# Cross-attention block: the opening, the steady round and the end of one instruction list put into a new order

## The chip, the core and the metric

The kernel runs on one core of a Trainium2 chip. Its engines work from separate instruction lists and meet only at semaphores: TensorE (PE in the profile; PEld is its loading of weights), VectorE (DVE), ScalarE (ACT) and GpSimd (POOL) compute, and SyncE (SP) issues nearly all DMAs. The metric is the device time of one execution in microseconds; less is better.

## The reference

64 sequences; each has 256 rows of text (512 wide) and 256 rows of audio (384 wide). All is float32.

```python
text_p  = einsum('bld,dh->blh', H_l, W_text) + b_text      # 256 x 512
audio_p = einsum('bsd,dh->bsh', H_a, W_audio) + b_audio    # 256 x 512
Q = layer_norm(text_p, g1, beta1)
K = layer_norm(audio_p, g2, beta2)
alpha = softmax(einsum('blh,bsh->bls', Q, K) / sqrt(512))  # 256 x 256
H = einsum('bls,bsh->blh', alpha, audio_p)
H = einsum('blh,hk->blk', H, W_out) + b_out
out = layer_norm(H + H_l, g_out, beta_out)
```

## The kernel before

**What is computed how.** The audio and output weights are folded into one matrix (wao), so that the context is taken from the raw audio rows: z = alpha times c, then y = z times wao. The layer norms' means are taken out of the weights ahead of time. The products are cut into blocks whose sums and differences save products: `Thirds` (3 x 3 blocks; 15 products of 171 columns in place of more) for the K projection and for y, `Fork` (2 x 2 blocks; 7 products of 256 columns) for the Q projection, and in the rounds from 3 on the same scheme for the scores (`score_part`). The sums of inputs that they need are made by GpSimd: `Sides` (csum for K, zsum for y, seven steps each, one by `add(1)`), `SumX` (xsum, four steps), `query_step` (qsum, four) and `key_step` (ksum, three). Sums of results are made in PSUM by VectorE and ScalarE between the products. One matmul instruction of the program stands as two in the trace.

**The rounds.** Work on one sequence is spread over several rounds of a loop. Round b handles the projections of b + 2 (`k2`, `q2`) and the first Q product of b + 3 (`q3`), the scores of b (`at`), the context of b - 1 (`last`, `context_one`) and of b - 2 (`old`, `context_two`), the output product of b - 2 (`old.o`, called `y`) and the last layer norm of b - 3 (`settled`). Transposes go through memory: rows are stored (`store`, `store_e`), read back as blocks of 32 x 32 (`fetch`, `fetch_e`, four DMAs each), and VectorE turns the blocks (`turn`, `turn_e`, `turn_x`, `turn_c`).

**The order is the program's.** The scheduler is set to manual: each engine, and SP's queue of DMAs, carries out its instructions in the order of the statements. An instruction waits for what it reads, and for the readers of what it overwrites; all behind it on its engine waits too.

**The order inside Thirds**, for K and for y alike: `one` (two products into N), `copy_n1` (ACT), `start_t` (DVE, writes T), `two` (into M), `three` (into T, so it waits for `start_t`), `copy_t` (ACT), `start_l0` and `start_l1` (DVE, read M, write L), `four` (into T, M, L), `take_m` and `start_u` (DVE, read M, write U), `five` (into N, then M, then U). K leaves PSUM by `copy_n`, `copy_u`, `leave_middle`, `leave_ends`, `leave`, `middle_d`, `middle_sum`; y by `plus_ends`, `plus_middle`, `plus_n0` and four row sums `last_10`, `last_11`, `last_00`, `last_01` (each ends with a READ_ACCUMULATOR). `seed` writes the bias into M ahead of `two`. The banks M, L, T/U and N exist once and are used in turn by K and y.

**The order inside Fork:** `Fork.seed` writes R (ACT), `one` into R, `after_one` copies it, `seven` into q2 (cleared by `Fork.clear`), `after_seven` copies that, `six` into R, `start_q3` and `step_r` (DVE), `five` into R, `after_five` (DVE, reads R), `two`, `three` (into R) and `four`. Then `square`, `scales_of` (logarithm and exponential) and `normalise` on ACT, `store` and `fetch`.

**Around the rounds.** Ahead of the loop stand the loading, the first projections of sequences 0 and 1 in plain form (`Projection`), the turning of the weights (`turn_weights`), the folding (`fold_multiply`, `fold_evict`, `fold_bias`), and the block sums of the weights (`weight_sums`, `third_weights`). The loop runs over b = 0 to 61; a list of single statements serves b = 3 to 60, while b = 0, 1, 2 and 61 go through a shared body with conditions, which calls whole groups (`after_one`, `rest`, `sum_x`, `leave_plus`). Behind the loop the last sequences are finished with plain products (`multiply`, `multiply_half`, `multiply_halves`, `evict`, `evict_halves`), and the last alphas are transposed on TensorE (`transpose_e`). The weights' and the matmuls' own lines: 548 (Thirds), 721 (Fork), 806 and 867 (scores), 945 (context), 431 (plain projections), 244 (folding); VectorE's two-operand sums in Thirds, Fork and the scores all stand at line 532, the row sums at 691, `shift` at 1144, `settle` at 1153.

Of the kernel before, what the change touches and what calls it, by code (L numbers as in the profile page):

```python
# [22 lines left out]
def kernel(  # L23
# [1156 lines left out]
    def add_bias(b):  # L1180
        xb = x_rows[b]
        for t in range(LT):
            nc.gpsimd.tensor_tensor(xb[:, t, :], xb[:, t, :], bao_sb, ALU.add)
# [5 lines left out]
    c_turn = RowTurn(c_0, AC, "cT")  # L1189
    x_turn = RowTurn(x_0, DC, "xT")  # L1190
    k[0] = Projection("k", 0, c_turn.T, wa_sb, ba_sb, AC, ST, bank[0:2])
    q[0] = Projection("q", 0, x_turn.T, wt_sb, bt_sb, DC, LT, bank[2:4])
    keep_busy(6)
    c_turn.tile(0)
    c_turn.tile(1)
    for t in range(ST):
        k[0].multiply(t, [0])
    k[0].multiply(0, range(1, AC))
    k[0].multiply(1, [1])
    x_turn.tile(0)  # L1200
    k[0].multiply(1, range(2, AC))
    x_turn.tile(1)
    war = []
    for a in range(AC):
        pool, tag = (work, "eT") if a else (once, "e")
        war.append(pool.tile([P, HC, P], F32, tag=tag, name=f"war_{a}"))
        arrange(war[a], wa_sb[:, a, :], HC, nc.gpsimd.tensor_copy)
    mean_wa = means(wa_sb, AC, "mwa")
    k[0].evict(0)
    centre(wa_sb, mean_wa, AC)  # L1210
    for chunks in ([0, 1], [2, 3]):
        for t in range(LT):
            q[0].multiply(t, chunks)
    ba_row = ba_sb.rearrange("p (o h) -> p o h", o=1)
    bt_row = bt_sb.rearrange("p (o h) -> p o h", o=1)
    k[0].evict(1)
    mean_ba = means(ba_row, 1, "mba")
    mean_wt = means(wt_sb, DC, "mwt")
    mean_bt = means(bt_row, 1, "mbt")
    cT[1] = turn_c(1)  # L1220
    k[0].scales()
    centre(ba_row, mean_ba, 1)
    centre(wt_sb, mean_wt, DC)
    centre(bt_row, mean_bt, 1)
    turn_weights(0, 2)
    k[0].normalise()
    k[0].store()
    load_c(2)
    k[0].fetch()
    load_x(2)  # L1230
    k[1] = Projection("k", 1, cT.pop(1), wa_sb, ba_sb, AC, ST, bank[4:6])
    for t in range(ST):
        k[1].multiply(t, range(AC))
    turn_weights(2, 2)
    wt_blocks = weight_sums(wt_sb, DC // 2, "wtsum")
    q[0].evict(0)
    q[0].evict(1)
    q[0].scales()
    xT[1] = turn_x(1)
    xs_1 = SumX(xT.pop(1), nc.vector)  # L1240
    xs_1.add(1)
    k[1].evict(0)
    k[1].evict(1)
    Fork.clear()
    xs_1.add(2)
    bt_step = const.tile([P, H2], F32, tag="bt_step", name="bt_step")
    nc.vector.tensor_tensor(bt_step, bt_sb[:, :H2], bt_sb[:, H2:], ALU.subtract)
    xs[1] = xs_1.add()
    cT[2] = turn_c(2)
    Fork.seed()  # L1250
    q[0].normalise()
    q[0].store()
    load_c(3)
    q[0].fetch()
    k[1].square()
    fold_multiply(0)
    g1_sb, be1_sb, g2_sb, be2_sb, bac_sb = take_columns()
    for v in (g2_sb, be2_sb):
        nc.vector.tensor_scalar(v, v, scale, None, ALU.mult)
    q[1] = Fork(1, xs.pop(1), wt_blocks)  # L1260
    q[1].one()
    q[1].seven()
    q[1].after_one()
    q[1].after_seven()
    wa_t = const.tile([P, 11, WP], F32, tag="wa_thirds", name="wa_thirds")
    third_weights(wa_sb, wa_t, [0])
    k[1].scales()
    wa_blocks = third_weights(wa_sb, wa_t, [3])
    cs[2] = Sides(cT.pop(2), "csum").add()
    ba_delta = third_bias(ba_sb, "ba_delta")  # L1270
    third_weights(wa_sb, wa_t, [1], nc.vector)
    fold_multiply(1, 0, 2)
    q[1].six()
    q[1].after_six()
    third_weights(wa_sb, wa_t, [4], nc.vector)
    fold_evict(0)
    Thirds.seed_with(ba_sb)
    k[1].normalise()
    k[1].store()
    load_x(3)  # L1280
    k[1].fetch()
    fold_multiply(1, 2, 4)
    fold_evict(1)
    q[1].five()
    q[1].after_five()
    xT[2] = turn_x(2)
    third_weights(wa_sb, wa_t, [2], nc.vector)
    part = bias_parts()
    bias_rest(part, 1, 3)
    folds.append(p_at.tile([P, H], F32, tag="at", name="ps_fold"))  # L1290
    fold_multiply(2, 0, 2)
    q[1].rest()
    q[1].square()
    q[1].scales()
    xs[2] = sum_x(xT.pop(2))
    q[1].normalise()
    q[1].store()
    q[1].fetch()
    wao_room = const.tile([P, HC * H], F32, tag="wo", name="wao_thirds")
    wao_t = wao_room[:, : 11 * WP].rearrange("p (n h) -> p n h", n=11)  # L1300

    def last_rows(b):
        x_rows[b] = blk.tile([P, LT, D], F32, tag="xq", name=f"x_{b}")
        nc.sync.dma_start(x_rows[b], x[b].rearrange("(t p) d -> p t d", p=P))
        c_rows[b] = blk.tile([P, ST, DA], F32, tag="cq", name=f"c_{b}")
        nc.sync.dma_start(c_rows[b], c[b].rearrange("(t p) d -> p t d", p=P))

    done = None
    for b in range(B - 2):
        at = att[b] = att.get(b) or Attention(b)  # L1310
        settled, old, last = att.pop(b - 3, None), att.get(b - 2), att.get(b - 1)
        three = b + 3 < B
        fast = b > 2 and three
        soon = b > 1
        if fast:
            k2 = k[b + 2] = Thirds("k", b + 2, cs.pop(b + 2), wa_blocks, ba_sb, ba_delta)
            q2 = q[b + 2]
# [45 lines left out]
            if b + 4 < B: load_c(b + 4)  # L1363
# [508 lines left out]
```

## Time and profile before

| | us |
|---|---|
| median of 3 runs (lowest to highest) | 1368.44 (1367.55 to 1368.47) |
| the profiled execution | 1367.78 |
| its span, first to last instruction | 1365.9 |
| TensorE busy | 1342.8 |
| VectorE, ScalarE, GpSimd busy | 1157.5, 1161.8, 1171.5 |
| share of the DMA engines' time in queue 1 | 84.5% |

A line of the timeline gives the start in us, the time from the first start to the last end, engine, source line, operation, what is written and read, the shape, and how many instructions were merged; in brackets the idle time of the engine before it and what ended it. A line of the waits gives who waited for whom: total us, times, longest. A line of the stages gives the stretch, its width, then for PE, PEld, DVE, ACT and POOL the busy time and the number of instructions, then the granted clock, the DMA share and GB/s. A line of the DMA issues ends with KB each and the median us from issue to landing. In a line of the groups stand, behind the count, busy us and mean ns of one, then the idle time ahead of them. Ends of matmuls are modelled, and in the timeline they overlap the next start.

### The profile page before, as it was taken

What the parts mean: (1) busy time and instruction counts of PE and PEld (TensorE: products, weight loads), DVE (VectorE), ACT (ScalarE), POOL (GpSimd) and SP (SyncE); (2) the same over time, 40 slices, a digit from 0 to 9 for tenths busy, and PEclk for the clock granted to TensorE, in tenths of its full rate; (3) what the DMA queues carried; (4) which work ended last, traced back from release to release, by engine and by line L of the source; (5) the groups of instructions that cost most, each with busy time, mean ns of one, the idle gap of its engine ahead of it and who ended that gap; (6) DMA issues with size and microseconds to landing.
All of it is one profiled execution on the core that took longest, in us unless ns stands there. A gap on an engine that the chain in (4) does not pass through costs nothing.

```text
span 1365.9 us, 28598 instructions
## 1 busy us (share of the span) xinstructions
PE 1342.8 (98%) x8125; PEld 1244.8 (91%) x8125; DVE 1157.5 (85%) x2733; ACT 1161.8 (85%) x3188; POOL 1171.5 (86%) x1838
## 2 busy tenths in 40 slices
PE   9999999999999999999999999999999999999997
PEld 5789999999999999999999999999999999999985
DVE  6758888888888888889888888888888888888857
ACT  5688988888888888888888888888888888888874
POOL 5669988989989889889899889899899889989844
PEclk9999999999999999999999999999999999999999
DMA  9786888988998898898888888898889899889772
GB/s 227 202 236 184 255 229 238 254 235 236 249 250 239 251 244 239 249 245 242 248 243 234 249 234 247 232 247 256 233 243 257 232 248 253 235 239 260 210 241 90
DMA packets 449107, 322.15 MB, mean 236 GB/s; under 512 B 153781, under 2 KB 381621, under 8 KB 448950
## 3 DMA queue, kind: packets, MB, share of 16 engines
q1 hardware_dynamic: 448854, 320.20, 84.5%
q8 instruction: 66, 1.08, 0.4%
q14 instruction: 91, 0.75, 0.2%
q10 hardware_dynamic: 96, 0.13, 0.0%
HBM read 203.57 MB, written 116.65 MB: 234 GB/s over the span
## 4 chain that ended last, share of the span: by engine, by line
PE 78%; DMA 7%; ACT 6%; DVE 3%; issue 2%; POOL 2%; SPq 1%; DVEq 0%; ACTq 0%; POOLq 0%
PE ps_f L721 23%; PE ps_m L548 13%; PE ps_sc L867 11%; PE ps_z L945 9%; PE ps_n L548 8%; PE ps_u L548 7%; PE ps_l L548 4%; DMA qd<-qr 2%; DMA kq<-kd 2%; DMA kd<-kr 1%; DMA qq<-qd 1%; ACT qr L787 1%; SPq L73 1%; ACT junk L777 1%; ACT junk L451 1%
## 5 line engine op out<-in xcount | busy, mean ns | idle before, releaser
L343 POOL TENSOR_TENSOR csum<-csum,cT 128x256 f32<-128x256 f32 x310 | 195.5, 640 | 9.9
L343 POOL TENSOR_TENSOR zsum<-zsum,zT 128x256 f32<-128x256 f32 x305 | 196.4, 653 | 5.3
L721 PE MATMUL ps_f<-wtsum,xsum 128*128 128x256 f32 x756 | 193.6, 379 | 0.5 <-DVE ps_f L532 0.5
L945 PE MATMUL ps_z<-eT,c 128*128 128x256 f32 x768 | 186.4, 379 | 0.2 <-ACT e L896 0.2
L945 PEld LDWEIGHTS ps_z<-eT,c 128*128 128x128 f32 x768 | 140.3, 190 | 14.1 <-ACT e L896 0.6
L721 PEld LDWEIGHTS ps_f<-wtsum,xsum 128*128 128x128 f32 x756 | 138.0, 190 | 15.1 <-DVE ps_f L532 1.2
L518 ACT ACTIVATE kT<-kT,columns 128x256 f32<-128x256 f32 x256 | 145.0, 596 | 2.8 <-DVE kT L511 1.5
L518 ACT ACTIVATE qT<-qT,columns 128x256 f32<-128x256 f32 x256 | 145.2, 593 | 2.2 <-DVE qT L76 2.2
L343 POOL TENSOR_TENSOR csum<-cT 128x256 f32<-128x256 f32 x124 | 98.6, 795 | 50.4 <-DVE cT L76 50.4
L721 PE MATMUL ps_f<-wt,xT 128*128 128x256 f32 x504 | 129.4, 379 | 0.6 <-ACT ps_f L713 0.6
L867 PE MATMUL ps_sc<-kT,qT 128*128 128x128 f32 x928 | 122.3, 275 | 0.0
L1153 DVE SCALAR_TENSOR_TENSOR yr<-yr,rstd,beo 128x512 f32<-128x512 f32 x120 | 119.6, 998 | 0.0
L849 POOL TENSOR_TENSOR ksum<-kT 128x512 f32<-128x512 f32 x58 | 73.9, 1275 | 53.0 <-ACT kT L518 53.0
L867 PEld LDWEIGHTS ps_sc<-kT,qT 128*128 128x128 f32 x928 | 116.6, 192 | 0.0
L867 PEld LDWEIGHTS ps_sc<-ksum,qsum 128*128 128x128 f32 x696 | 100.6, 191 | 6.0
L532 DVE TENSOR_TENSOR ps_l<-ps_m,t 128x171 f32<-128x171 f32 x248 | 85.3, 344 | 24.4 <-PE ps_m L548 12.9
L867 PE MATMUL ps_sc<-ksum,qsum 128*128 128x128 f32 x696 | 105.9, 275 | 0.0
L511 DVE STREAM_TRANSPOSE kT<-kq 128x512 f32<-128x512 f32 x122 | 85.4, 701 | 23.3 <-DMA kq<-kd 20.7
L777 ACT ACTIVATE junk<-ps_f 128x512 f32<-128x512 f32 x126 | 74.3, 590 | 36.2 <-PE ps_f L721 35.9
L1144 DVE SCALAR_TENSOR_TENSOR yr<-yr,nm,go 128x512 f32<-128x512 f32 x124 | 102.9, 831 | 1.0 <-ACT junk L1025 1.0
L721 PEld LDWEIGHTS ps_f<-wt,xT 128*128 128x128 f32 x504 | 92.9, 190 | 11.4 <-ACT ps_f L713 0.9
L76 DVE STREAM_TRANSPOSE qT<-qq 128x1024 f32<-128x1024 f32 x64 | 79.5, 1242 | 18.2 <-DMA qq<-qd 17.4
(265 smaller groups left out, 4127.9 us busy)
## 6 DMA issues: line engine op xcount, KB each, us to landing
kd<-kr SPq DMA_DIRECT2D x64, 512.0 KB, 3.1
kq<-kd SPq DMA_DIRECT2D x256, 128.0 KB, 3.8
qd<-qr SPq DMA_DIRECT2D x64, 512.0 KB, 5.2
qq<-qd SPq DMA_DIRECT2D x256, 128.0 KB, 3.7
xq<-in_x_dram SPq DMA_DIRECT2D x252, 128.0 KB, 5.0
x<-in_x_dram SPq DMA_DIRECT2D x63, 512.0 KB, 4.4
out_dram<-yr SPq DMA_DIRECT2D x62, 512.0 KB, 5.5
cq<-in_ctx_dram SPq DMA_DIRECT2D x252, 96.0 KB, 2.3
```

The lines of the kernel that those rows point to most:

```text
L76: nc.vector.transpose(dst.rearrange("p k (b j) -> p b k j", j=SQ), src.rearrange("p b (k i) -> p b k i", k=chunks),)
L343: nc.gpsimd.tensor_tensor(*step)
L511: nc.vector.transpose(self.T.rearrange("p k (q t j) -> p t q k j", t=self.nt, j=SQ)[:, t], self.sq[:, t * NQ : (t + 1) * NQ].rearrange("p ...
L518: nc.scalar.activation(self.T[:, k, :], self.T[:, k, :], AF.Identity, bias=bet[:, k : k + 1], scale=gam[:, k : k + 1],)
L532: nc.vector.tensor_tensor(o, i0, i1, op)
L548: nc.tensor.matmul(place, lhsT=self.sides.of[n], rhs=self.weights[n], start=(n == 14), stop=True, skip_group_check=True,)
L721: nc.tensor.matmul(place, lhsT=side, rhs=w, start=False, stop=True, skip_group_check=True)
L777: nc.scalar.activation(junk, fork[t], AF.Square, scale=1.0 / math.sqrt(H), accum_out=self.var[:, t : t + 1],)
L867: nc.tensor.matmul(self.place(t, m), lhsT=self.qsides[n][:, c], rhs=self.ksides[n][:, c], start=False, stop=True, skip_group_check=True,)
L945: nc.tensor.matmul(ps, lhsT=c_rows[self.b][:, s, bass.ts(j, P)], rhs=self.eT[:, s, :], start=start, stop=(s == ST - 1), skip_group_check=True,
L1144: nc.vector.scalar_tensor_tensor(row, row, self.nm[:, t : t + 1], go_sb, ALU.add, ALU.mult)
L1153: nc.vector.scalar_tensor_tensor(self.y[:, t, :], self.y[:, t, :], self.r[t], beo_sb, ALU.mult, ALU.add)
```

## The change

No operation, size or buffer is changed in the rounds; statements are put into another order. (1) All that stands ahead of round 3 is one list of single statements, in which the work of the plain start and of rounds 0, 1 and 2 is interleaved; groups are taken apart (`xs[2].add(1)` four times in place of `sum_x`, `score(0, 1)` ... in place of `score(0, 8)`, `bias_rest` and `fold_multiply` step by step). (2) The steady round, b = 3 to 60, has a new order. (3) Round 61 and the end are one list as well, with `add_bias` taken tile by tile. Of the first part (names with _0, _1, _2 belong to rounds 0 to 2):

```diff
+    fold_multiply(2, 0, 1)
+    q[1].three()
...
+    k2_0.one()
+    k2_0.copy_n1()
+    k2_0.start_t()
...
+    q[1].two()
+    load_c(3)
+    q[1].four()
...
+    fold_multiply(2, 1, 2)
...
+    fold_multiply(2, 2, 3)
...
+    fold_multiply(1, 3, 4)
+    Fork.seed()
+    k[1].store()
+    k2_0.two()
+    k2_0.three()
...
+    q2_0.one()
...
+    k2_1.one()
...
+    at_0.score(7, 8)
+    scales_of(q2_0, k2_0, var_0)
+    k2_1.copy_n1()
...
+    k2_1.start_t()
...
+    k2_1.three()
...
+    at_1.score(7, 8)
+    last_1.context_one()
+    k2_2.two()
+    Fork.seed()
...
+    q2_2.one()
```

The steady round, old (whole in the listing above, from `if fast:`) and new, in the new one all that the prediction speaks of:

```diff
-            k2.three()
-            k2.copy_t()
...
-            settled.shift(0)
-            q2.five()
...
-            k[b + 1].turn([0])
-            k2.leave_middle()
-            k2.leave_ends()
-            k2.leave()
-            q2.after_five()
...
-            y.start_t()
-            q2.three()
...
-            k2.store()
-            load_c_rows(b)
...
-            q2.store()
+        k2.one()
+        old.context_two(0); old.context_two(1)
+        k2.copy_n1()
+        at.affine_queries(3)
+        if b + 4 < B: load_c(b + 4)
+        cT[b + 3] = turn_c(b + 3)
+        old.copy_two()
+        q2.seven()
...
+        cs[b + 3].add(1)
+        k2.start_t()
+        k2.three()
...
+        load_x_rows(b - 1)
...
+        old.start_products(n=1)
...
+        q2.start_q3()
+        if done: done.store()
...
+        k2.take_m()
...
+        k2.start_u()
+        k2.five()
+        k2.copy_n()
+        q[b + 1].turn()
+        at.score_part(1, 7)
+        q2.step_r()
+        q2.five()
+        last.fetch_e()
...
+        k2.leave_ends()
...
+        k[b + 1].turn([0])
...
+        k2.leave_middle()
+        k2.leave()
+        y.one()
+        q2.after_five()
+        load_c_rows(b)
+        k[b + 1].turn([1])
+        y.copy_n1()
+        at.copy_p7()
+        k2.middle_sum()
+        y.start_t()
+        y.two()
+        at.query_step(2)
+        k2.square(var[:, 2:], [0])
+        at.copy_p1()
+        settled.shift(0)
...
+        q2.four()
+        y.three()
...
+        at.score_part(6)
+        if b + 4 < B: load_x(b + 4)
+        at.add_p7(0)
+        y.copy_t()
+        settled.shift(1)
+        q2.two()
+        q2.three()
...
+        settled.settle(1)
...
+        at.add_p7(1)
+        y.four()
+        scales_of(q2, k2, var)
...
+        settled.settle(0)
+        q2.normalise([0])
+        at.score_part(2)
+        last.turn_e()
...
+        y.take_m()
+        at.score_part(4)
+        at.score_part(3)
+        y.start_u()
+        at.maxima()
+        q2.normalise([1])
+        y.five()
...
+        y.plus_ends(x_old)
+        Fork.seed()
...
+        k2.normalise([1])
+        k2.normalise([0])
+        last.context_one()
...
+        y.plus_middle(x_old, 1)
+        at.exponentials([1])
+        y.last_11()
+        y.last_01(x_old)
+        q2.store()
+        y.plus_n0()
...
+        y.last_10()
...
+        k2.store()
...
+        q3.one()
...
+        q2.fetch()
...
+        k2.fetch()
+        y.last_00()
+        at.store_e()
```

Of the end:

```diff
+    last.o.one()
...
+    at.multiply(0, bank[5])
+    last.o.start_t()
+    last.o.three()
...
+    at.multiply_half(1, bank[4], 0)
...
+    at.multiply_half(1, bank[4], 1)
...
+    end.context_one()
...
+    end.copy_one()
+    last.totals()
+    last.deviation(0)
+    end.copy_two()
+    end.start_output()
+    end.multiply(0, bank[0])
```

More of the change, by code (lines that the diff above doesn't have):

```diff
@@ L1223 @@
-    centre(wt_sb, mean_wt, DC)
-    centre(bt_row, mean_bt, 1)
-    turn_weights(0, 2)
-    k[0].normalise()
-    k[0].store()
[L1228 to L1236, printed above, removed]
+    ba_row = ba_sb.rearrange('p (o h) -> p o h', o=1)
+    mean_ba = means(ba_row, 1, 'mba')
@@ L1278 @@
[L1278 to L1292, printed above, removed]
+    q[1].six()
+    q[0].store()
+    g1_sb, be1_sb, g2_sb, be2_sb, bac_sb = take_columns()
+    fold_multiply(0, 3, 4)
@@ L1297 @@
-    q[1].store()
-    q[1].fetch()
[L1299 to L1306, printed above, removed]
@@ new lines @@
+    at_1.score(0, 1)
+    k2_1.copy_u()
+    k2_2 = k[4] = Thirds('k', 4, cs.pop(4), wa_blocks, ba_sb, ba_delta)
+    k2_2.one()
+    at_1.affine_queries(2)
+    at_1.affine_queries(3)
+    last_1.store_e()
+    k2_1.leave_middle()
+    at_1.affine_keys(1)
+    k2_2.copy_n1()
+    q2_1.after_five()
+    q2_1.three()
+    beo_sb = row(beta_out, 'beo')
+    k2_1.middle_d()
+    at_1.score(1, 2)
+    q2_1.two()
+    k[2].fetch()
+    k2_1.leave_ends()
+    at_1.affine_keys(2)
+    at_1.score(2, 3)
```

1313 lines of the change are left out of this document (780 added, 533 removed).

## The prediction

> **What bounds the kernel now.** I read the page's head first, then the busy times by stage, then the timeline of TensorE, and last who waits for whom.
>
> ```profile
> span 1365.9 us, 28598 instructions
> ...
> PE 1342.8 (98%) x8125; PEld 1244.8 (91%) x8125; DVE 1157.5 (85%) x2733; ACT 1161.8 (85%) x3188; POOL 1171.5 (86%) x1838
> ```
> ```profile
> 7.00:102.00 95.00, 89.36 (x391) 66.32 (x390) 64.17 (x127) 68.39 (x173) 60.34 (x102) 1.00 0.87 225
> 102.00:1296.00 1194.00, 1191.07 (x7427) 1126.03 (x7426) 1045.17 (x2493) 1047.88 (x2901) 1079.69 (x1682) 1.00 0.87 241
> 1296.00:1357.00 61.00, 56.87 (x293) 48.36 (x291) 41.37 (x102) 41.27 (x107) 27.42 (x42) 1.00 0.53 166
> ```
> TensorE (the first number behind the width) is the bound in every stage, at full granted clock. The reader is to see that there is little to win: the change keeps every matmul, so only TensorE's pauses, its start and what follows its last matmul can shrink. How large they are is seen in its timeline:
>
> ```profile
> 102.11 0.45 PE L548 MATMUL ps_n<-wa,csum 128*128 128x171 f32 x2
> ...
> 277.92 1.13 PE L721 MATMUL ps_f<-wt,xsum 128*128 128x256 f32 x4 [0.54 <-DVE ps_f L532]
> ...
> 607.37 1.03 PE L721 MATMUL ps_f<-wtsum,xT 128*128 128x256 f32 x4
> 608.23 0.61 PE L867 MATMUL ps_sc<-ksum,qsum 128*128 128x128 f32 x4
> ...
> 617.40 0.31 PE L548 MATMUL ps_n<-wa,csum 128*128 128x171 f32 x1
> ...
> 637.86 0.31 PE L548 MATMUL ps_n<-wa,csum 128*128 128x171 f32 x1
> ...
> 1295.86 0.31 PE L548 MATMUL ps_n<-wa,csum 128*128 128x171 f32 x1
> ...
> 1355.75 1.46 PE L1107 MATMUL ps_u<-wao,zT 128*128 128x256 f32 x6
> ```
> A round begins with `k2.one()` (ps_n<-wa,csum). From 617.40 to 637.86 is 20.46 us without a pause. The 58 rounds written as one list (b = 3 to 60) run from 102.11 to 1295.86, that is 1193.75; at 20.46 they would be 1186.7, so **7.1 us** are lost in them, on some rounds only. A pause costs more than the idle time shown: four products are shown as 1.03 but the next starts 0.86 after them (0.17 of drain), and behind a pause they take 1.13 (0.10 of refill), so some 0.25 is added to each. Ahead of round 3 the idle time is 95.00 - 89.36 = 5.6, in nine pauses, so **7.9 us** are lost; in the last stage 61.00 - 56.87 = 4.1 in five pauses, **5.4 us**. Behind the last matmul (1355.75 + 1.46 = 1357.2) stand 8.7 us.
>
> ```profile
> PE ps_u L548 <- DVE ps_u L532: 7.9, 7, 1.5
> ```
> ```profile
> 1311.35 0.53 PE L548 MATMUL ps_u<-wao_thirds,zsum 128*128 128x171 f32 x2 [1.40 <-DVE ps_u L532]
> ...
> 1327.85 0.53 PE L548 MATMUL ps_u<-wao_thirds,zsum 128*128 128x171 f32 x2 [1.53 <-DVE ps_u L532]
> ...
> 1339.55 0.53 PE L548 MATMUL ps_u<-wao_thirds,csum 128*128 128x171 f32 x2 [0.64 <-DVE ps_u L532]
> ```
> Seven of the pauses are one wait: `three()` needs `start_t`, which needs ACT's `copy_n1`, which needs `one()`. Three lie in the tail (1.40 + 1.53 + 0.64 = 3.6), so the other four, 4.3, lie in the first rounds.
>
> **The first three rounds.** Up to the products of `q[0]` TensorE's list is the old one. The new lists put each `one`, `copy_n1`, `start_t` well ahead of its `three`: between `k2_0.one` and `k2_0.three` stand two products, three folds and `two` (about 4.9 us of TensorE, a 256-wide product of four matmuls being 0.86), between `k2_1.one` and its `three` eight score steps, and so on. The copy (0.3), `start_t` (0.34) and two hops need about 1 us once ACT is free. All four waits go: 4.3 + 4 x 0.25 = 5.3. The remaining 2.6 (five pauses) I neither credit nor charge in detail: the new order also has places without reserve. `Fork.seed` must wait for squares, logarithm, exponential and normalise behind `four`, about 3 us of ACT; the order leaves 3.4 us of TensorE there in round 0 and over 4 in the others. And `last_1.context_one` now comes in round 1 ahead of the fork's first product, behind a store and a fetch of e. Bounds: from all 7.9 gone to 2 us worse; value taken -5.4, since the waits named are surely broken up and the new ones look short.
>
> **The steady round.** Its pauses (the row at 277.92 is one) are `q2.three` waiting for `after_five`, which stands on DVE behind the first half of the kT transpose:
>
> ```profile
> DVE kT L511 <- DMA kq<-kd: 20.7, 24, 1.8
> ...
> DVE qT L76 <- DMA qq<-qd: 17.4, 34, 1.0
> ```
> ```profile
> SPq L73 <- DMA qd<-qr: 48.7, 62, 3.5
> ```
> ```profile
> kd<-kr SPq DMA_DIRECT2D x64, 512.0 KB, 3.1
> kq<-kd SPq DMA_DIRECT2D x256, 128.0 KB, 3.8
> qd<-qr SPq DMA_DIRECT2D x64, 512.0 KB, 5.2
> qq<-qd SPq DMA_DIRECT2D x256, 128.0 KB, 3.7
> ```
> ```profile
> 618.61 1.90 SPq L73 DMA_DIRECT2D kq<-kd  x4
> ...
> 621.37 1.92 SPq L73 DMA_DIRECT2D qq<-qd  x4
> 624.49 2.98 SPq L73 DMA_DIRECT2D eq<-ed  x4
> ...
> 635.84 0.38 SPq L489 DMA_DIRECT2D kd<-kr  x1
> 636.32 0.42 SPq L101 DMA_DIRECT2D c<-in_ctx_dram  x1
> 636.79 0.87 SPq L489 DMA_DIRECT2D qd<-qr  x1
> ```
> ```profile
> 623.83 0.71 DVE L511 STREAM_TRANSPOSE kT<-kq 128x512 f32<-128x512 f32 x1
> ...
> 626.77 1.25 DVE L76 STREAM_TRANSPOSE qT<-qq 128x1024 f32<-128x1024 f32 x1
> ...
> 629.41 0.30 DVE L532 TENSOR_TENSOR ps_sc<-ps_sc,sc 128x128 f32<-128x128 f32 x1 [0.54 <-PE ps_sc L867]
> ```
> Counting from the round's start (617.40): the k fetch is issued from 1.2 to 3.1, lands some 3.8 later, and is wanted at 6.4, so nothing is in reserve. DVE is late by up to 1.8, TensorE stands from about 0.5 on. The new order turns q first (at 5.7, behind `start_u`), the first half of k at 7.7, and moves `q2.three` from 9.3 to 12.3. `load_c_rows` leaves its place between the two stores. `y.three` (10.7) becomes the first product to feel a late k; its `start_t` ends at about 10.2, and DVE idles 0.4 ahead of `after_five`. So k may land at 8.3 instead of 6.9, 1.4 later, for the same issue times: that covers nearly all lateness seen. I take 1.0 of the 7.1 as left, a gain of 6.1; bounds 0 to 7.1 for this cause.
>
> The moves that I cost at nothing are these. On SP the list becomes `load_c`, `load_x_rows`, the output store, `last.fetch_e`, `load_c_rows`, `load_x`, the q and k stores, the q and k fetches, `store_e`; it is the same 26 transfers. SP waits for the q store's landing about where it waited before, with only the k fetch and the e store behind it, and the rows that the five loads bring are used a round later: a round of 20.46 us hides them. If that cover went, `turn_c`, now the first long DVE work of a round, would hold `start_t` and `three` one for one. The e fetch (now at 7.1, 624.49) stays near 7 to 10, since the e store still goes out at about 3, and `turn_e` comes at about 15: some 4 us cover it. On ACT the q rows' normalise moves ahead of k's, and `Fork.seed` ahead of both k halves, which only eases the next `q3.one`; `copy_p1` moves behind a square and must end ahead of the sixth score part (11.0), about 10.7 by my layout, the smallest reserve on ACT. On POOL one csum step moves ahead of the zsum chain:
>
> ```profile
> L343 POOL TENSOR_TENSOR zsum<-zsum,zT 128x256 f32<-128x256 f32 x305 | 196.4, 653 | 5.3
> ```
> A step is 0.65 at the mean, so the fifth zsum step ends at about 7.5 and `y.one` starts at 8.7: covered by 1 us, and a shortfall would count in full.
>
> With these durations laid end to end, two places are narrow. First, `last_10` moves behind `last_11` and `last_01`; it frees the bank that the next `k2.one` writes:
>
> ```profile
> 635.25 0.51 DVE L532 TENSOR_TENSOR n<-ps_m,x 128x342 f32<-128x342 f32 x1 [0.54 <-PE ps_m L548]
> ...
> 636.79 0.51 DVE L691 SCALAR_TENSOR_TENSOR yr<-ps_n,n 128x342 f32<-128x342 f32 x1
> 637.23 0.08 DVE L691 DVE_READ_ACCUMULATOR yr<-ps_n,n 128x1 f32 x1
> ```
> From 17.85: two sums (0.43 and 0.24), two row sums of 0.44 and 0.42, `plus_n0` 0.37, `last_10` 0.34: free at 20.1. TensorE wants it about 0.22 ahead of 20.46, so 0.1 is left; with 0.12 of hand-over at each row sum it would be 0.1 late. Taken at 0, bound 58 x 0.1 = 6 us. The second is the third rival below.
>
> **The tail.** All three `three` waits get other products between (for `last.o` a whole `at.multiply(0)`, 2.6 us): -(3.6 + 3 x 0.25) = -4.3. Against it, `at.multiply_half`, which until now filled the time of the last `copy_two`, is moved ahead of `end.context_one`, and `end.copy_two` still stands on ACT behind `last.deviation(0)`; TensorE then has nothing until `end.multiply(0)`. Copy and hops alone are 0.6; if the deviation is late, 1.3 or more. I charge 1.0, and 0.8 for the longer DVE list ahead of the last evictions. Net -2.5; bounds -4.5 to +1. The 8.7 us behind the last matmul keep the same steps.
>
> **Sum.** The profiled execution took 1367.78, 1.9 more than its span; the median shown is 1368.44, 0.66 above it. 1367.78 - 5.4 - 6.1 - 2.5 = 1353.8, and as a median **1354.4 us**.
>
> **The rivals.** *The q fetch comes too late (slower).* q is turned 3.7 us earlier in the round (626.77 is 9.4), ahead of `step_r`, and `q2.five` (7.8) needs that. The new ACT order finishes q at about 16.5, ahead of k, so the store goes out at 16.55 instead of 19.4. With the store's landing time L, the last of four fetches is issued 1.5 behind it and lands 3.7 later: 1.3 + L in the next round. At L = 3.1, as for kd into an idle queue, that is 4.4: in time. At L = 5.2, as for qd now, it is 6.5: 0.8 late, of which 0.3 is absorbed, and 58 x 0.5 = 29 us are lost: 1383. It decides from L = 4.7 on. For it speaks that the row says 5.2; against, that those 5.2 stand behind kd and the c rows, which the new order puts behind q.
>
> *The rounds win nothing* (another hop takes the place of `after_five`, or the bank above is late): 1354.4 + 6.1 = 1360.5. For it speak the 0.1 and 0.3 us reserves; against, that most rounds already run at 20.46 with reserves like these.
>
> *Lengthened DVE work (slower).* `settle(1)`, `settle(0)` and `turn_e` now stand ahead of `take_m` and `start_u`, which the third pair of `y.five` (17.0) needs by 16.75.
>
> ```profile
> 618.06 1.01 DVE L1153 SCALAR_TENSOR_TENSOR yr<-yr,rstd,beo 128x512 f32<-128x512 f32 x1
> ...
> 630.62 1.21 DVE L1144 SCALAR_TENSOR_TENSOR yr<-yr,nm,go 128x512 f32<-128x512 f32 x1
> ...
> 631.96 0.73 DVE L1153 SCALAR_TENSOR_TENSOR yr<-yr,rstd,beo 128x512 f32<-128x512 f32 x1
> ```
> The same instruction takes 0.73 or 1.01, and the shift 0.74 to 1.21, depending on what runs beside it. From `add_p7(0)` at 11.7 (629.41 is 12.0; the sixth part comes 0.3 earlier) the chain ends at 16.2 with the short times and at 17.2 with the long ones: 0.4 late, 58 x 0.4 = 23 us, 1377. POOL should idle from about 12.7 until `key_step(0)`, so I expect it short. The Trainium skill ("SBUF — State Buffer") states that VectorE and GpSimd share one port pair under an exclusive lock, and that a VectorE instruction with two SBUF inputs contends with a GpSimd instruction that reads SBUF. The two durations of one instruction above agree; which engine was ahead the row does not say.
>
> *The start wins nothing* (the e fetch or the seeds replace the old waits): 1354.4 + 5.4 = 1359.8.
>
> **How the numbers follow.** The forecast gets 0.56, rounds without gain 0.12, start without gain 0.10, both together (about 1366 to 1368) 0.06, late q 0.09, lengthened DVE 0.07. A difference under 0.2% (2.7 us) can't be told from none. Faster: 0.56 + 0.12 + 0.10 = 0.78; same 0.06; slower 0.16. The likeliest case has 1349 to 1360; to hold 8 in 10 the range reaches over the partial cases, to a slight loss: 1349 to 1372.
>
> **What would show it.** Right: rounds of 20.46 from first to last, no `three` wait on ps_u above 0.3, kq and qq waits of DVE gone or harmless, a new wait for the last zT copy near the end. Wrong: a wait that comes back in every round: ps_f behind `step_r` (late q), ps_m in `y.five` (long DVE work), ps_n at the round's start (bank), each visible as a longer round; or pauses in the first 100 us of the old sum.

## The result, and the profile after

The changed kernel takes **1348.77 us** (median of 4 runs, 1348.47 to 1349.4), the kernel before beside it 1368.45: a ratio of 0.9857 with the interval 0.984 to 0.9874, 19.7 us less. Forecast were 1354.4 with a range of 1349 to 1372; the time lies 0.2 below the range. The direction came as forecast, the gain was 5.6 larger; of the reasons given, part held and part did not.

The profiled execution took 1349.4, and its page begins:

```profile
span 1347.6 us, 28668 instructions
...
PE 1337.4 (99%) x8125; PEld 1246.1 (92%) x8125; DVE 1114.9 (83%) x2733; ACT 1163.0 (86%) x3188; POOL 1140.3 (85%) x1838
```

The stretches (width, then busy time of PE, PEld, DVE, ACT, POOL), cut where the three lists meet, and the rows of TensorE's timeline at these cuts and at its end:

```profile
7.00:96.00 89.00, 88.11 (x391) 66.41 (x390) 61.57 (x127) 67.95 (x173) 61.41 (x104) 1.00 0.91 231
96.00:1284.17 1188.17, 1187.81 (x7426) 1126.70 (x7426) 1007.34 (x2496) 1050.03 (x2901) 1048.07 (x1681) 1.00 0.90 244
1284.17:1340.27 56.10, 56.10 (x293) 48.73 (x291) 40.59 (x101) 41.40 (x109) 27.58 (x42) 1.00 0.56 172
```
```profile
96.01 0.74 PE L548 MATMUL ps_n<-wa,csum 128*128 128x171 f32 x4
...
1284.16 0.59 PE L945 MATMUL ps_z<-eT,c 128*128 128x256 f32 x2
...
1338.81 1.46 PE L1107 MATMUL ps_u<-wao,zT 128*128 128x256 f32 x6
```

The instructions of TensorE are the same 8125, its granted clock is 1.00 as before, and in the last stretch it has no idle time at all (56.10 of 56.10). Round 3 begins at 96.01 (102.11 before), the list of round 61 at 1284.16 (1295.86), the last matmul ends at 1338.81 + 1.46 = 1340.27 (1357.2). That gives each stage its share:

| stage | before | after | difference | forecast |
|---|---|---|---|---|
| up to round 3 | 102.1 | 96.0 | -6.1 | -5.4 |
| 58 steady rounds | 1193.75 | 1188.15 | -5.6 | -6.1 |
| round 61 to the last matmul | 61.35 | 56.1 | -5.2 | } -2.5 |
| behind the last matmul | 8.7 | 7.3 | -1.4 | } |
| span | 1365.9 | 1347.6 | -18.3 | -14.0 |

Round 3 can also begin earlier than in this trace: seven traces of kernels with this list ahead of round 3 have its start at 94.07 to 96.08, at the mean 95.1.

Who waits for whom, first TensorE's list, then VectorE's waits for the fetches of e and k, and the DMA issues:

```profile
PE ps_f L187 <- POOL ones L111: 1.6, 1, 1.6
PE ps_m L244 <- issue: 0.6, 1, 0.6
...
PE ps_m L548 <- DVE ps_u L532: 0.2, 1, 0.2
```
```profile
DVE eT L76 <- DMA eq<-ed: 7.6, 7, 4.2
...
DVE kT L511 <- DMA kq<-kd: 0.6, 1, 0.6
```
```profile
kd<-kr SPq DMA_DIRECT2D x64, 512.0 KB, 2.9
qd<-qr SPq DMA_DIRECT2D x64, 512.0 KB, 2.8
kq<-kd SPq DMA_DIRECT2D x256, 128.0 KB, 3.1
qq<-qd SPq DMA_DIRECT2D x256, 128.0 KB, 2.7
...
eq<-ed SPq DMA_DIRECT2D x244, 64.0 KB, 5.0
```

The first row is the wait for a constant at the start, as before. The wait of ps_u ahead of `three`, 7.9 in seven pauses before, is gone. So are VectorE's waits for kq and qq (20.7 and 17.4): the 0.6 that is left for kq lies ahead of round 3. What is new is small: VectorE waits for the fetch of e seven times, once for 4.2 ahead of round 3 and six times in the steady rounds, for 3.3 together. The longest of the six, 0.96 at 869.68, reaches TensorE as the pause of 0.23 on ps_m in `y.five`, at 871.04. Of the 58 steady rounds, three of those with such a wait are longer than 20.46, by 0.16, 0.31 and 0.50. The q store lands in 2.8 where it took 5.2.

### The profile page after: what moved, and what is told of

It reads as the page before. It is cut to its first block, busy times and chain, and to the rows that moved or that the text cites. A ratio compares the mean times of both kernels' runs of the same rounds, so it can differ in the third digit from the quotient of the medians.

```text
span 1347.6 us, 28668 instructions
## 1 busy us (share of the span) xinstructions
PE 1337.4 (99%) x8125; PEld 1246.1 (92%) x8125; DVE 1114.9 (83%) x2733; ACT 1163.0 (86%) x3188; POOL 1140.3 (85%) x1838
## 4 chain that ended last, share of the span: by engine, by line
PE 98%; DVE 0%; SPq 0%; DMA 0%; issue 0%; ACT 0%; POOL 0%; DVEq 0%; POOLq 0%
PE ps_f L721 28%; PE ps_m L548 16%; PE ps_sc L867 13%; PE ps_z L945 12%; PE ps_n L548 11%; PE ps_u L548 8%; PE ps_l L548 5%; PE ps_sc L806 2%; PE ps_f L431 0%; DMA eq<-ed 0%; SPq L73 0%; PE ps_m L244 0%; PE ps_u L431 0%; PE ps_fold L244 0%; PE ps_l L244 0%; PE ps_n L431 0%
## 5 line engine op out<-in xcount | busy, mean ns | idle before, releaser
L343 POOL TENSOR_TENSOR csum<-csum,cT 128x256 f32<-128x256 f32 x310 | 220.4, 712 | 9.7
L343 POOL TENSOR_TENSOR zsum<-zsum,zT 128x256 f32<-128x256 f32 x305 | 167.5, 566 | 0.5
L1144 DVE SCALAR_TENSOR_TENSOR yr<-yr,nm,go 128x512 f32<-128x512 f32 x124 | 116.9, 943 | 0.7 <-ACT junk L1008 0.7
L867 PEld LDWEIGHTS ps_sc<-ksum,qsum 128*128 128x128 f32 x696 | 97.9, 191 | 3.1
L1008 ACT ACTIVATE junk<-yr,nm 128x512 f32<-128x512 f32 x124 | 89.8, 724 | 5.5
L343 POOL TENSOR_TENSOR csum<-cT 128x256 f32<-128x256 f32 x124 | 73.8, 595 | 23.0 <-DVE cT L76 22.8
L852 POOL TENSOR_TENSOR qsum<-qT 128x256 f32<-128x256 f32 x116 | 84.8, 731 | 6.1
L1153 DVE SCALAR_TENSOR_TENSOR yr<-yr,rstd,beo 128x512 f32<-128x512 f32 x120 | 89.4, 745 | 0.0
L314 POOL TENSOR_TENSOR xsum<-xT 128x256 f32<-128x256 f32 x124 | 89.0, 739 | 0.2 <-DVE xT L76 0.2
```

Of the source, the lines that this page charges most:

```text
L314: self.engine.tensor_tensor(*step)
L343: nc.gpsimd.tensor_tensor(*step)
L852: nc.gpsimd.tensor_tensor(*self.steps[n])
L867: nc.tensor.matmul(self.place(t, m), lhsT=self.qsides[n][:, c], rhs=self.ksides[n][:, c], start=False, stop=True, skip_group_check=True,)
L1008: nc.scalar.activation(junk, self.y[:, t, :], AF.Square, bias=self.nm[:, t : t + 1], accum_out=self.ssq[:, t : t + 1],)
L1144: nc.vector.scalar_tensor_tensor(row, row, self.nm[:, t : t + 1], go_sb, ALU.add, ALU.mult)
```

## The experiments

Three runs take one part of the change each, with the other two in the old order. The fourth undoes one suspected cause in the kernel before. Times are medians; the length of a stage is read from the one profiled execution of each kernel.

**The opening alone.** The new list ahead of round 3, then the old steady rounds and end.

> Everything ahead of round 3 in the new order, the steady rounds and the last stage in the old one. My theory (the three parts are independent, and each removes its own pauses of TensorE): ahead of round 3 the two traces differ by 6.2 us (102.1 against 96.0 us for the start of round 3), so this kernel is 5 to 7 us faster than before, about 1362.3, a ratio of 0.9955, and its 58 steady rounds still lose about 7 us. Rival (the parts lean on each other: the old steady round begins with whatever the new opening hands it, so a wait that left the opening returns in the first old rounds): under 3 us faster, with new pauses in rounds 3 to 5.

Measured 1360.17, ratio 0.9943 (0.9926 to 0.996): 8.3 less than the 1368.52 of before. Its stretch from 7 to 102 us:

```profile
7.00:102.00 95.00, 95.00 (x435) 73.40 (x434) 66.74 (x140) 73.86 (x190) 67.31 (x114) 1.00 0.92 235
```

TensorE has no idle time left there, and round 3 begins at 94.80, 7.3 earlier than before. No new pauses follow in the old rounds (1193.0 for the 58, 1193.75 before): the rival falls. The gain is above the 5 to 7 expected, in part because the expectation went by the opening of the changed kernel's trace, one of the slowest. Every pause of this stage is gone, not only the four that the prediction credited.

**The steady rounds alone.**

> Only the 58 steady rounds in the new order; the opening, round 61 and the last stage in the old one. My theory: the steady rounds lose 7.1 us before and 1.9 after, so this kernel is 4.5 to 6 us faster, about 1363.2, a ratio of 0.9962, with the waits of the kT and qT transposes for kq and qq gone from the DVE list and the lateness of `last_10` and of the long DVE work costing nothing. Rival (the steady round's gain in the changed kernel came from the opening's order of the queues and not from its own list): under 2 us faster, with the waits for kq still there.

Measured 1362.43, ratio 0.9958 (0.9943 to 0.9973): 6.1 less. VectorE's list has no wait for kq and none for qq any more; the one fetch for which it still waits is that of e:

```profile
DVE eT L76 <- DMA eq<-ed: 0.4, 2, 0.3
```

The theory holds, the gain being at its upper end: the new rounds win without the new opening.

**The end alone.**

> Only round 61 and the last stage in the new order; the opening and the 58 steady rounds in the old one. My theory: the last stage loses 5.4 us of TensorE before and 0.1 after, and what stands behind the last matmul is 8.7 before and 7.3 after, so this kernel is 6.6 us faster (6 to 7.5), about 1361.9, a ratio of 0.9952. Rival (the figure of the prediction, that a copy behind the last deviation holds TensorE up by 1.0 and the longer VectorE list by 0.8, masked in the one profile by chance): about 2.5 us faster.

Measured 1365.98 (1364.66 to 1368.46 in 10 runs), ratio 0.9986 (0.9977 to 0.9996): 2.5 less, the very number of the rival; the 6 to 7.5 of the theory were missed. The trace shows why it is no proof of the rival. A row of TensorE's timeline and one of VectorE's waits in round 61 of this kernel:

```profile
1307.94 0.85 PE L548 MATMUL ps_m<-wao,zsum 128*128 128x171 f32 x4 [2.95 <-ACT ps_m L562]
```
```profile
DVE qT L76 <- DMA qq<-qd: 4.4, 1, 4.4
```

The new list turns q early in round 61, but the old round ahead of it still fetches q late. VectorE stands for 4.4 with the sums of K behind it, ScalarE's write of the bias into M waits for these, and TensorE waits for that: 2.95. It is a price of the seam between two orders, which the whole change does not pay.

**The old kernel with one load moved.** In its steady round, only this:

```diff
             k2.store()
-            load_c_rows(b)
...
             q2.fetch()
+            load_c_rows(b)
             y.last_00()
```

> The kernel before with one transfer issue moved in the steady round: the load of the context rows, which stood between the store of k and the store of q, comes behind the fetch of q. Theory (the load of 512 KB between the two stores makes the q store, and with it both fetches, land late, and that lateness is what the steady pauses are): 3 to 5 us faster, a ratio of about 0.997, and the idle time of VectorE at kT<-kq falls from 20.7 us to under 8. Rival (the lateness is the place at which the order of VectorE wants k, 6.4 to 6.9 us into the round, and not the load): less than 1 us of change, ratio 0.9995 to 1.0005, and the idle time at kT<-kq stays between 15 and 25 us.

Measured 1361.56, ratio 0.9953 (0.9938 to 0.9968): 7.0 less than before, as much as all of the new steady round brings (6.1 alone; the two intervals overlap). The stretch of its steady rounds, VectorE's only wait of any size for the two fetches, and its DMA issues:

```profile
102.11:1289.00 1186.89, 1186.62 (x7422) 1126.06 (x7421) 1041.52 (x2488) 1044.27 (x2899) 1064.93 (x1682) 1.00 0.88 242
```
```profile
DVE qT L76 <- DMA qq<-qd: 1.8, 6, 0.5
```
```profile
kq<-kd SPq DMA_DIRECT2D x256, 128.0 KB, 2.7
qd<-qr SPq DMA_DIRECT2D x64, 512.0 KB, 3.8
```

TensorE is idle for 0.3 in 1187, and the 58 rounds take 1187.60 in place of 1193.75. In the new order they take 1187.14 to 1188.85 in seven traces, so beyond the moved load no gain of the new round can be told. The wait for kq is out of the list, k's fetch lands in 2.7 (3.8 before) and q's store in 3.8 (5.2). So the lateness of k came from this load (of 384 KB, not 512) between the stores; with it moved, the old place of the turn is late enough.

The next three start from the changed kernel. **The load put back** between its stores:

```diff
         q2.after_five()
-        load_c_rows(b)
...
         q2.store()
+        load_c_rows(b)
         y.plus_n0()
```

> The changed kernel with the load of the context rows put back between the two stores of the steady round (behind the q store, ahead of the k store). Theory (in the old order that load was the whole cause of the steady pauses; the new order was saved by moving it as much as by turning k later): the k store lands about 5.2 us behind its issue instead of 2.9, as the q store did behind the same load in the kernel before, so k lands near 8.0 us into the round where VectorE wants it at 7.6; part of the rounds pause again, 1.5 to 8 us slower than the changed kernel (about 1350 to 1357), with VectorE idle at kT<-kq for more than 5 us in total. Rival (the later turn of k, at 7.6 and not 6.4, is what removed the pauses, and covers the load too): within 0.7 us of the changed kernel.

Measured 1357.61 (1354.88 to 1358.73), 8.8 slower than the changed kernel. VectorE's waits for the fetches, TensorE's wait in the rounds, and the k store:

```profile
DVE eT L76 <- DMA eq<-ed: 24.5, 31, 4.0
...
DVE kT L511 <- DMA kq<-kd: 5.6, 13, 1.3
```
```profile
PE ps_m L548 <- DVE ps_u L532: 4.5, 7, 1.2
```
```profile
kd<-kr SPq DMA_DIRECT2D x64, 512.0 KB, 4.5
```

The store behind the load is again the slow one (k's now, 4.5). The loss is a little above the theory's 8; in the traces the steady rounds take 1195.57, 7.4 more than in the changed kernel and 1.8 more than in the kernel before. The way is as the theory had it only in part: k is late 13 times (once of them ahead of round 3), but the pauses of TensorE stand at `y.five`, since SP now waits for the k store in every round (64.8 in 58 waits, 3.4 in six without the load), so that it fetches e later too, and `turn_e` (late 31 times, once ahead of round 3) stands ahead of `take_m` and `start_u`. The new order tolerates this load no better than the old one did.

**The last copy first.** `end.copy_two` ahead of `last.totals` and `last.deviation(0)`.

> The changed kernel with the last `end.copy_two` ahead of `last.totals` and `last.deviation(0)` on ScalarE. Theory (the product `end.multiply(0)` starts with the two chunks that `copy_one` delivers and reaches the third only some 1.7 us later, so the copy was never late): no change, within 0.5 us, and the pause ahead of the product stays under 0.2. Rival (the prediction's: TensorE waits there for a copy behind a deviation, 1.0): 0.7 to 1.0 faster.

Measured 1347.81 (1347.61 to 1348.47), 1.0 less. By the time alone that is the rival. The rows of ScalarE and TensorE, first of the changed kernel, then of this one:

```profile
1334.20 0.59 ACT L961 COPY zT<-ps_z 128x512 f32<-128x512 f32 x1 [3.17 <-POOL nm L990]
...
1334.84 2.84 PE L1042 MATMUL ps_m<-wao,zT 128*128 128x512 f32 x6
1335.40 0.36 ACT L964 COPY zT<-ps_z 128x256 f32<-128x256 f32 x1
```
```profile
1333.05 0.59 ACT L961 COPY zT<-ps_z 128x512 f32<-128x512 f32 x1 [3.17 <-POOL nm L990]
...
1333.69 2.84 PE L1042 MATMUL ps_m<-wao,zT 128*128 128x512 f32 x6
1333.86 0.37 ACT L964 COPY zT<-ps_z 128x256 f32<-128x256 f32 x1 [0.22 <-PE ps_z L945]
```

In both, the product begins 0.64 after the start of `copy_one` and lasts 2.84, whether `copy_two` (L964) ends 0.54 after the product's start (1333.86 + 0.37) or 0.92 after it (1335.40 + 0.36): only the fifth and sixth of its six instructions read the third chunk, and the fifth starts 1.82 behind the first. The copy was never late. From the first product of round 61's list to the end of the last matmul both traces take the same 56.11. Of the 0.9 by which the two profiled executions differ (1348.47 and 1349.4), 0.85 lie ahead of round 3, which began at 95.16 in this trace and at 96.01 in that of the changed kernel.

**The last settle beside GpSimd.** `at.settle(1)` behind `end.evict(0)`.

> The changed kernel with the last `at.settle(1)` of VectorE moved behind `end.evict(0)`, to where GpSimd is adding a row to the last output (`last.lift_rows`); the number of VectorE's instructions ahead of the last evictions stays the same. Theory (in the kernel before, this one instruction ran beside that GpSimd work and took 1.57 us instead of 0.75, which is why VectorE reached the last eviction 1.2 behind the last matmul): it takes 1.4 to 1.6 again, the last eviction starts 0.6 to 0.8 behind the last matmul instead of 0.04, and the kernel is 0.6 to 0.9 slower. Rival (what matters is only how many instructions stand ahead of the evictions): it takes 0.75, no change, within 0.3.

Measured 1348.48, 0.3 less: in the time no difference can be told. The rows of VectorE and GpSimd, first of the changed kernel, then of this one:

```profile
1337.17 0.75 DVE L1153 SCALAR_TENSOR_TENSOR y<-y,rone,beo 128x512 f32<-128x512 f32 x1
...
1340.31 0.48 DVE L1121 SCALAR_TENSOR_TENSOR y<-ps_u,rden,x 128x256 f32<-128x256 f32 x1 [0.21 <-PE ps_u L1107]
...
1338.14 2.80 POOL L1162 TENSOR_TENSOR yr<-yr,beo 128x512 f32<-128x512 f32 x2 [1.50 <-ACT yr L1158]
```
```profile
1333.38 1.27 POOL L1162 TENSOR_TENSOR yr<-yr,beo 128x512 f32<-128x512 f32 x1
...
1337.42 2.95 POOL L1162 TENSOR_TENSOR yr<-yr,beo 128x512 f32<-128x512 f32 x2 [1.49 <-ACT yr L1158]
1337.78 1.47 DVE L1153 SCALAR_TENSOR_TENSOR y<-y,rone,beo 128x512 f32<-128x512 f32 x1
1338.09 1.46 PE L1107 MATMUL ps_u<-wao,zT 128*128 128x256 f32 x6
...
1340.02 0.47 DVE L1121 SCALAR_TENSOR_TENSOR y<-ps_u,rden,x 128x256 f32<-128x256 f32 x1
```

The same instruction takes 1.47 beside GpSimd's row sums and 0.75 alone, as expected, and the last eviction now starts 0.47 behind the last matmul (1340.02 against 1339.55) in place of 0.04. The cost, 0.4, is half of what was expected, because VectorE had 0.21 of idle time to give, and it drowns in the differences of the opening. The first of the two GpSimd instructions, 1.27 long, ends at 1338.69 and the settle at 1339.25, 0.56 later: it did most of its work behind it. The second, which starts while the settle still runs, lasts 1.72 (1338.65 to 1340.37) in place of 1.27. The Trainium skill ("SBUF — State Buffer", "SBUF: two separate sides") states that the pair of ports goes to whichever starts first, for the whole instruction; this trace agrees.

**The end behind the new rounds.** The test that the run of the end alone could not give: new opening and rounds, old end.

> New opening and new steady rounds; round 61 and the last stage in the old order. The last stage alone was only 2.5 us faster than before, and its trace showed one pause of 3.1 where the q that the new list turns early had not yet been fetched by the old rounds. Theory (that pause is a handover between two orders, and the new last stage is worth 6.6 behind the new rounds): this kernel is 6.6 us slower than the changed kernel, about 1355.4. Rival (the last stage is worth the 2.5 of the prediction): about 1351.3.

Measured 1353.41, ratio 0.9883 (0.9865 to 0.9901): 4.6 slower than the changed kernel. By the traces the end is worth more: this one reached round 3 at 94.59, 1.4 ahead of the changed kernel's profiled run. Its first and last rows of TensorE in question:

```profile
1281.73 0.74 PE L548 MATMUL ps_n<-wa,csum 128*128 128x171 f32 x4
...
1340.98 1.46 PE L1107 MATMUL ps_u<-wao,zT 128*128 128x256 f32 x6
```

From the first product of round 61 to the last matmul's end are 60.7 us (56.1 in the changed kernel), and from there to the end of the span, 1351.1, 8.7 (7.3): together 6.0, near the 6.6 of the theory and far from 2.5. The time alone, 4.6, lies between the two; it is the stage that decides, because the openings of the two traces differ by 1.4.

**The opening, counted backwards.** Old opening, new rounds and end.

> Old opening; new steady rounds and new last stage. Theory (all the pauses ahead of round 3 go with the new opening, 7.3 us of TensorE by the run of the opening alone, and the old opening hands zsum to the first new round about 0.5 to 1.2 late): 6.5 to 8.5 us slower than the changed kernel, 1355.3 to 1357.3. Rival (the prediction's size, 5.4, and no handover): about 1354.2.

Measured 1356.23, ratio 0.9902 (0.9884 to 0.992): 7.5 slower than the changed kernel, inside the theory's bounds. In the trace round 3 begins at 102.02, 6.0 later than in the changed kernel's, and the first two steady rounds are 1.2 and 0.2 longer than 20.46: a handover is there, though only 0.2 of it is shown as a wait for zsum.

**One `three` moved close again.** `k2_0.three()` right behind `k2_0.start_t()`.

> The changed kernel with `k2_0.three()` of the opening moved up to right behind `k2_0.start_t()`, as close as in the kernel before. Theory (the pauses of the opening are the chain one, copy, start_t, three, and what removed them is the work between): a pause of 0.9 to 1.5 of TensorE at ps_u appears at that one place, ahead of round 3 nothing else changes, 1.0 to 1.7 us slower than the changed kernel, about 1350. Rival (the new opening gains because its transfers and the turns of q and k are earlier, not because of the distance): no pause over 0.3 there.

Measured 1348.5 (1348.44 to 1350.05): the median shows nothing. The trace has the pause at this place, and no other on ps_u:

```profile
38.91 0.53 PE L548 MATMUL ps_u<-wa_thirds,csum 128*128 128x171 f32 x2 [0.92 <-DVE ps_u L532]
```

It is a pause as in the kernel before (the four were 0.78 to 1.40 there): at this one of the four places the distance between `start_t` and `three` is what removes it, and the rival falls. The expected 1.0 to 1.7 did not come: round 3 begins at 96.01 in this trace and in that of the changed kernel, which had lost 0.64 at its first fold instead. That 1 us does not show in the median sets the limit of what single times can tell here.

**The q fetch behind the k fetch.**

```diff
-        q2.fetch()
+        k2.fetch()
         if b + 4 < B: att[b + 1].key_step(2)
-        k2.fetch()
+        q2.fetch()
         y.last_00()
```

> The changed kernel with the fetch of k ahead of the fetch of q in the steady round, so that the q fetch stands behind the wait for the k store: it is issued from about 2.9 to 4.8 us into the round instead of from -0.9 to 1.0. This is the prediction's rival of a late q, made on purpose. Theory (q is wanted at 5.7 and has about 1.5 to 2 of reserve): it lands at about 7.5, VectorE waits for it in every round and most of the lateness reaches TensorE: 40 to 110 us slower than the changed kernel, 1390 to 1460, with idle time at qT<-qq of over 60 us. Rival (the transpose of q can be late by as much, since step_r and the k transpose behind it have reserve of their own): under 10 us slower.

Measured 1451.35, ratio 1.0594 (1.0562 to 1.0625), 102.6 slower than the changed kernel. The waits, TensorE's and VectorE's, and from one round of the DMA queue the q store and the q fetch:

```profile
PE ps_f L721 <- DVE ps_f L532: 80.3, 58, 2.6
```
```profile
DVE qT L76 <- DMA qq<-qd: 70.7, 36, 3.2
```
```profile
1046.48 0.38 SPq L489 DMA_DIRECT2D qd<-qr  x1
...
1052.75 1.88 SPq L73 DMA_DIRECT2D qq<-qd  x4
```

The q fetch goes out 6 us behind its store, because the k fetch and its wait for the k store stand ahead of it. VectorE waits for it 2.0 at the mean (70.7 / 36; ahead of the other 22 turns it waits as long, 42.2 in all, which the profile puts down to GpSimd instructions), and a round loses 1.8 (102.6 / 58): nearly all of the lateness reaches TensorE. The way that the prediction's rival of the late q described is real.

**A version below both.** `last.turn_e` goes behind `y.start_u`, and one product is moved ahead of the opening's first fold.

```diff
+    k[1].multiply(1, [2])
     fold_multiply(0, 0, 1)
...
-    k[1].multiply(1, [2])
...
-        last.turn_e()
...
         y.start_u()
+        last.turn_e()
```

> An attempt at a version that beats both: the changed kernel with `last.turn_e` behind `y.start_u` in the steady round, so that a late fetch of e no longer holds `take_m` up, and with the product `k[1].multiply(1, [2])` ahead of the first fold of the opening, so that the fold waits 0.4 later for its weights. Theory (three steady rounds lose 0.3 to 0.5 each because VectorE waits for eq ahead of `take_m`, and the first fold lost 0.8 in that run): 1.0 to 2.0 faster than the changed kernel, about 1347.3, and no pause of `y.five` at ps_u. Rival (context_one, which needs the transpose of e, or the exponentials behind it, take over the lateness): within 0.5 or slower.

Measured **1346.6** (1346.48 to 1346.83), ratio 0.9843 (0.9829 to 0.9858), 2.2 below the changed kernel and a little more than expected. All four runs lie below all four of the changed kernel; the intervals of the two ratios overlap. TensorE's whole list of waits is the wait for the first constant (the row `PE ps_f L187` as above), and VectorE's six waits for e in the steady rounds are gone. Which of the two moves won how much is not shown: round 3 begins at 94.18 and the 58 rounds take 1187.11, and without the moves the least were 94.07 and 1187.14.

## Why the prediction was right in its direction, and where it failed

**The bound.** That TensorE is the bound and no product changes was right. Of the 18.3 that the span lost, 16.9 lie ahead of the end of TensorE's last matmul and are its pauses, 1.4 lie behind it. The 0.25 that a pause costs beside its idle time was a little high: 0.18 in the opening alone (7.3 won for 5.6 of idle time in nine pauses), 0.22 in the last stage (5.2 for 4.1 in five).

**The opening** (-5.4 forecast, -6.1 measured; -7.3 with this part alone). The four waits of `three` went, as forecast, and the one put back shows the mechanism of that one. But the other 2.6, neither credited nor charged, went nearly whole as well: in the run of the opening alone TensorE has no idle time there. The places without reserve that were named cost at most 0.2 in any trace.

**The steady round** (-6.1 forecast, -5.6 measured). The size is right; of the reason, only half. Late k was the cause, and the later turn of k was taken for the remedy, the move of the load for a side effect. The runs show that the load was the remedy: moving it alone gives 7.0, and the new order without that move is 8.8 slower and wins nothing in the rounds, though k is turned at the same later place there. Of the two narrow places `last_10` cost nothing. At `take_m` and `start_u` ahead of `y.five` lies 1.0 of the 1.5 that the rounds still lose, through `turn_e`, to which the prediction gave 4 us of cover at no cost. It did not ask whether the landing time of the e fetch would stay, which in the kernel before was

```profile
eq<-ed SPq DMA_DIRECT2D x244, 64.0 KB, 2.2
```

In the new order this fetch is issued behind the load of c, a load of x rows and the output store, and it lands in 5.0: the last of the four, issued at about 9.6 of a round, arrives at 14.6, against a turn at about 15. In six rounds that left no cover. (The list of SP in the prediction has four loads, not five; nothing hangs on it.) The lengthened DVE work did not occur: the settles became shorter, as the groups show (behind the count: busy us, mean ns of one, idle time ahead), first before, then after:

```profile
L1153 DVE SCALAR_TENSOR_TENSOR yr<-yr,rstd,beo 128x512 f32<-128x512 f32 x120 | 119.6, 998 | 0.0
```
```profile
L1153 DVE SCALAR_TENSOR_TENSOR yr<-yr,rstd,beo 128x512 f32<-128x512 f32 x120 | 89.4, 745 | 0.0
```

**The tail is the step that failed** (net -2.5 forecast, -6.6 measured; it makes 4.1 of the 4.4 that are missing between the forecast sum and the profiled run). It is also why the time fell below the range: the lower end, 1349, is about the best case of all three stages at once (7.9, 7.1 and 4.5 less give 1348.9), and only the tail went beyond its own best case, 4.5. All the pauses of the stage went, 5.2, of which the prediction had credited the three waits of `three` with 4.3, leaving out two small ones; and nothing was given back. The 1.0 charged for `end.copy_two` ("TensorE then has nothing until end.multiply(0)") was 0: the product starts on the two chunks that `copy_one` delivers. The 0.8 for the longer DVE list was 0 (VectorE begins the last eviction 0.04 behind the last matmul), and "the 8.7 us behind the last matmul keep the same steps" missed that VectorE began the last eviction 1.2 behind the last matmul's end (1357.2), because its last settle ran beside GpSimd. Rows of GpSimd and VectorE of the kernel before:

```profile
1355.02 3.07 POOL L1162 TENSOR_TENSOR yr<-yr,beo 128x512 f32<-128x512 f32 x2
1355.39 1.57 DVE L1153 SCALAR_TENSOR_TENSOR y<-y,rone,beo 128x512 f32<-128x512 f32 x1
...
1358.40 0.47 DVE L1121 SCALAR_TENSOR_TENSOR y<-ps_u,rden,x 128x256 f32<-128x256 f32 x1
```

In the new order it doesn't, and 1.4 more is won. The move of the settle showed the doubling, and 0.4 of the 1.4; what makes the rest was not tried by itself. Both could have been read off the trace of before: what each chunk of a product needs, and one instruction shown twice as long as its equals.

**The rivals.** The late q hinged on L, the landing time of the q store, with 4.7 as the point; L is 2.8, so it stayed out. That a late q would reach TensorE nearly whole, the run that made it late shows. The rounds and the start both won. Neither of the two ways in which it would have been slower occurred.

**Parts do not add.** Alone, the three parts give 8.35 + 6.09 + 2.54 = 17.0; together 19.7. The pause at the seam of round 61 (2.95) is about as large as the difference; that it makes the whole of it is argued, not shown.

## What to carry to other kernels

Where a fetch is late, look at what stands between its store and the store ahead of it in the same queue before you reorder the compute: here one moved load was worth as much as a whole new order of the round. Then look at what stands behind the load in its new place: its landing time will change too. Before you charge a wait for a copy, see which chunk of the product reads it, and look for instructions that last twice as long as their equals: they show who runs beside them. Parts of a hand-written order are not safely priced by swapping them in one by one: here the end won 2.5 behind the old rounds and 6.0 behind the new ones, with a wait of 2.95 where the two orders met.

## What the runs showed of the hardware that had not been expected

A load of 384 KB issued between two stores of 512 KB lengthened the landing of the second one from 3.8 to 5.2 us, and that of the fetch of k, behind both stores, from 2.7 to 3.8. Moved ahead of the fetch of e, the same load went with a longer landing of that fetch, 4.1 in place of 2.2. By which way a load delays its neighbours no run here separates.

The opening is not the same from run to run. With one and the same list ahead of round 3, round 3 began at 94.07, 94.59, 94.80, 94.90, 95.16, 96.01 and 96.08 in seven traces. In that of 96.01, the changed kernel's, TensorE stood ahead of the first fold:

```profile
26.63 1.10 PE L244 MATMUL ps_m<-wo,waT 128*128 128x512 f32 x2 [0.64 <-issue]
```
```profile
17.46 1.87 SPq L118 DMA_DIRECT2D wo<-in_L_xattn_W_out_dram  x4
```
```profile
wo<-in_L_xattn_W_out_dram SPq DMA_DIRECT2D x4, 256.0 KB, 7.3
```

The last of the four loads of wo is issued at about 19 and lands 7.3 later, near the 26.63 at which the product starts. TensorE's lists have this pause with 1.1 in the trace of 96.08, 0.3 in that of 95.16 and 0.4 in that of 94.90, and none in the three earliest, so it goes with the spread. That it is a wait for this load is argued from these rows and was not tried by itself; that the version above, with one product moved ahead of the fold, has no pause there proves nothing, since the same list without the move has none in three of seven traces.
